# A graph layer and a small network on one core: a sort run earlier and in shorter pieces, weights on another queue, a finer last unit

## The chip, the core and the metric

The kernel runs on one core of a Trainium2 chip. The core has five engines with instruction streams of their own: TensorE (PE) multiplies matrices, VectorE (DVE) and ScalarE (ACT) work elementwise, GpSimd (POOL) prepares indirect memory accesses here, and SyncE (SP) only issues DMAs. An engine executes its instructions strictly in order, and waits at one whose inputs are not there. DMAs can be issued from SP's, ACT's and POOL's queues and are carried out by 16 DMA engines.

The metric is the time of one execution on the device in microseconds (us). For the kernel before, three runs gave 1962.46, 1963.09 and 1964.54: the median is 1963.09 us.

## What is computed

```python
def gnn(x, weight, row, col, vals):
    h = jnp.einsum('nf,ef->ne', x, weight)
    return jax.ops.segment_sum(vals[:, None] * h[col], row, num_segments=8192)

def ffn(x_bd, W, b):                      # W: 7 layers of 160 x 160
    mask = (x_bd[..., 0] >= 0.5) & (x_bd[..., 1] >= 0.5)
    ...                                   # two 4-bit numbers per row read from columns 64 to 111
    for i in range(7):
        h = jnp.einsum('bspd,ed->bspe', h, W[i]) + b[i]
        if i < 6: h = jax.nn.relu(h)
    ...                                   # one result per position, rounded, clipped to 0..15
    return x_bd with 2 * one_hot(result) added in columns 128 to 159 where mask

x = x + gnn(layernorm(x), L0_gnn_weight, src, dst, edge_weight)
x = x + ffn(layernorm(x)[None], L0_ffn_W, L0_ffn_b)[0]
```

x has 8192 rows of 512 floats; there are 131072 edges with a source row, a target row and a weight. For each edge one row of h, chosen by dst, is multiplied by the weight and summed into row src. The edges arrive sorted by dst, but the sum goes by src, so the kernel has to sort them by blocks of 128 rows of src itself.

## The kernel before

The 8192 rows are 64 blocks of 128. The work has three stages, and the order of PE, DVE and ACT is written out by hand with Python generators: each `yield` marks a place where another stream's instructions may be put in.

**Heads and first sort.** `project()` makes h block by block (a "head"). Two blocks of x come in by one DMA; `scale` takes mean and variance on DVE (L431, L432), the reciprocal deviation on ACT and DVE (L183, L184) and scales on ACT (L437); `turn` transposes on PE (L446) with a copy on ACT (L448); four matmuls (L464) and a copy (L466) give h, which SP stores to DRAM two blocks at a time (L468). `order(part)` sorts the edges of one part: for each chunk of edges, `chunk` works out a one-hot of the block (`hot`, L238), its running counts (L246, L248, L251, L252), the rank by PE (L257, L261), the slot (`at`, L265), and puts the edges into cells by matmuls (`blocks`, L274; `put`, L278; L289). After seven chunks for part 0 or nine for part 1, `squeeze` moves the filled cells together in ten rounds (L351 to L359, all on DVE but one copy), then PE transposes the result into the tables `at_dst`, `at_row` and `at_w` (L393, L395). A head is followed by 1.25 steps of the first sort, from head 5 on.

**Part 0 with the second sort.** Each block takes 6 tiles of 128 edges in part 0 and 11 in part 1: 384 and 704 tiles in all. For each tile POOL gathers 128 rows of h by an indirect DMA (L723) into `g`, DVE makes a weighted one-hot `hot` (L734, seven batches of four tiles ahead), and PE multiplies them into `p_g` (L750). A tiny matmul for each batch, the "join" into `p_j` (L748), reads one element of each of the four gathered tiles. `g` has six buffers of four tiles. A finished block is added to x on DVE (L768) and stored. After every fourth tile one step of the second sort follows.

**Part 1 with the network.** The blocks continue with 11 tiles each; the sum is added to the stored rows (L807) and the network `ffn` runs over units of eight blocks, one step after every fifth tile. It gathers the rows that need it into 128 columns and takes six layers (L523 to L534 on PE, L506 on DVE, L509 on ACT) and an output. Then eight instructions on ACT scale the unit's rows (L630), two on DVE add the result (L651), and SP stores 2 MB (L654).

At the start ACT issues the DMA for the graph weight (L153), then those of the network's weights (L165 to L173), and copies some of them to their places (L174 to L179) before its first instruction of a head.

Of the kernel before, what the change touches and what calls it, by code (L numbers as in the profile page):

```python
# [24 lines left out]
OPVAL = 2 + 27  # L25
# [8 lines left out]
def tile_gnn_ffn(  # L34
# [49 lines left out]
    GS = 4  # L84
    assert E % P == 0 and D == 512 and NB == 64 and N <= 1 << DSTS and LOW + BITS <= 31
# [79 lines left out]
    nc.scalar.dma_start(w_a, ffn_wT[:, :P, :].rearrange("l d e -> d l e"))  # L165
    for g in range(NG):
        gs = slice(GB * g, GB * (g + 1))
        nc.scalar.dma_start(w_b[gs], ffn_wT[:, P:, :].rearrange("l d e -> d l e"))
        for i, d in enumerate(GE_IN):
            nc.scalar.dma_start(w_in[GB * g + i : GB * g + i + 1, 0, :], ffn_wT[0, d : d + 1, :])  # L170
        nc.scalar.dma_start(b_b[gs], ffn_bT[P:, :])
    nc.scalar.dma_start(b_a, ffn_bT[:P, :])
    nc.scalar.dma_start(b_out, ffn_bT[RESULT : RESULT + 1, L - 1 : L].to_broadcast([P, 1]))  # L173
    nc.scalar.copy(wo_a[:, 0, 0:1], w_a[:, L - 1, RESULT : RESULT + 1])  # L174
    nc.scalar.copy(wo_b[:, 0, 0:1], w_b[:, L - 1, RESULT : RESULT + 1])
    for g in range(NG):
        gs = slice(GB * g, GB * (g + 1))
        nc.scalar.copy(w_z[gs, 1:, g, :], w_b[gs, 1 : L - 1, 0:P])
        nc.scalar.copy(w_z[GB * g : GB * g + 3, 0, g, :], w_in[GB * g : GB * g + 3, 0, 0:P])  # L179

    def rstd_of(pool, var_ap, n, name):
        r = pool.tile([P, n], F32, name=name)
        nc.scalar.activation(r, var_ap, AF.Sqrt, bias=eps)  # L183
        nc.vector.reciprocal(r, r)  # L184
        return r

# [25 lines left out]

    with tc.tile_pool(name="ld", bufs=1) as ld:
# [21 lines left out]
    def chunk(ck, ps_c, q, col):  # L235

        hot = ck.tile([P, GC, NB, GQ], BF16, name="hot")
        nc.vector.tensor_tensor(  # L238
            hot, each.rearrange("p (o b) g -> p o b g", o=1).to_broadcast([P, GC, NB, GQ]),
            blk[:, q].rearrange("p c (o g) -> p c o g", o=1).to_broadcast([P, GC, NB, GQ]),  # L240
            OP.is_equal)
        yield
# [6 lines left out]
        yield  # L249
        for c in range(1, GC):  # L250
            nc.vector.tensor_tensor(cum[:, c], cum[:, c - 1], hot[:, c - 1], OP.add)  # L251
        nc.vector.tensor_tensor(cum, cum, hot, OP.mult)  # L252
        yield
        p_rank = ps_c.tile([P, GC, NB // GC, GQ], F32, name="p_rank")
        nb = NB // GC
        for i in range(GC):
            nc.tensor.matmul(p_rank, eye, cum[:, :, i * nb : (i + 1) * nb, :], start=(i == 0),  # L257
                             stop=(i == GC - 1))
        yield
# [5 lines left out]
        nc.vector.tensor_tensor(  # L265
            at.rearrange("p n h s -> p n (h s)"),
            lots.rearrange("p (o h) s -> p o (h s)", o=1).to_broadcast([P, CG, CAP]),
            slot.to_broadcast([P, CG, CAP]), OP.is_equal)
        p_c = None
        for c0 in range(0, GC, SUB):  # L270
            cg = slice(c0 * GQ, (c0 + SUB) * GQ)
            n = SUB * GQ
            blocks = ck.tile([P, SUB, GQ, NB], F32, name="blocks", bufs=2)
            nc.scalar.copy(blocks, hot[:, c0 : c0 + SUB].rearrange("p c b g -> p c g b"))  # L274
            put = ck.tile([P, n, 2, 2, HALF], F32, name="put", bufs=2)
            for i, val in enumerate((val_a, val_w)):
                v = val[:, q, c0 : c0 + SUB, :].rearrange("p c (g a b) -> p (c g) a b", a=1, b=1)
                nc.vector.tensor_tensor(put[:, :, :, i, :], at[:, cg],  # L278
                                        v.to_broadcast([P, n, 2, HALF]), OP.mult)
            yield  # L280
# [4 lines left out]
            for k in range(n):  # L285
                c, g = divmod(k, GQ)
                last = c0 + SUB == GC and k == n - 1
# [7 lines left out]
    def squeeze(part, sq, ps_q):  # L295
# [7 lines left out]
        nc.vector.tensor_tensor_scan(dist, free, free, 0.0, op0=OP.add, op1=OP.max)  # L303
# [8 lines left out]
        yield  # L312
# [5 lines left out]
        nc.vector.tensor_tensor(dist, dist, free, OP.mult)  # L318
        nc.vector.tensor_copy(word, cells_a[:, :ROW])
        yield  # L320
        nc.vector.tensor_copy(far, dist)
        nc.vector.scalar_tensor_tensor(word, far, LOW, word, op0=OP.logical_shift_left,
# [158 lines left out]
    for _ in heads:  # L481
        pass
    for _ in first:
        pass
# [542 lines left out]
```

## Time and profile before

| what | us |
|---|---|
| median of three runs | 1963.09 |
| the profiled execution, its own time | 1969.51 |
| its span, first to last instruction | 1967.7 |
| PE busy | 1686.7 (86%) |
| DVE busy | 982.7 (50%) |
| ACT busy | 388.9 (20%) |
| POOL busy | 1143.2 (58%) |

Rows of the profile name an engine, a line, an operation and the tiles (out<-in). A group has its count, its busy time and mean duration in ns, then the engine's idle time before such instructions and what ended it. The page also cuts the span in 40 slices; a digit is the busy share in tenths:

```profile
PE   3999999667989899996687789898998989899994
DVE  2555655865556565659923333534434443434412
POOL 2000000007778787778877777777777777777750
```

The first nine slices, of 49 us each, are the heads with the first sort; then come some twelve of part 0, and the rest is part 1. POOL's work, apart from setting constants in the first slice, is the gathers alone. Issuing a DMA from SP or ACT is not counted as busy.

### The profile page before, as it was taken

How to read it: one execution, taken by the hardware profiler on the slowest of the kernel's cores; microseconds unless marked ns; L12 is line 12 of the kernel's file. 1: busy time of each engine (PE TensorE's matmuls, PEld its weight loads, DVE VectorE, ACT ScalarE, POOL GpSimd, SP SyncE). 2: the span in 40 equal slices, each digit the busy share in tenths (PEclk: the TensorE clock that was granted, in tenths of full speed). 3: DMA queues.
4: the chain of work that ended last, by engine and by line, in shares of the span. 5: the costliest groups of instructions: out<-in, count | busy, mean ns of one | idle time of the engine just before them, and what ended most of it. 6: DMA issues, size and time to landing. Idle time of an engine off the chain costs nothing. (4 is left out here: it accounts for less than half of the span.)

```text
span 1967.7 us, 24257 instructions
## 1 busy us (share of the span) xinstructions
PE 1686.7 (86%) x9389; PEld 806.8 (41%) x9389; DVE 982.7 (50%) x2318; ACT 388.9 (20%) x513; POOL 1143.2 (58%) x1115
## 2 busy tenths in 40 slices
PE   3999999667989899996687789898998989899994
PEld 1555555323445454442233334343433434343442
DVE  2555655865556565659923333534434443434412
ACT  3545555331112111111100001010010101001012
POOL 2000000007778787778877777777777777777750
PEclk9999999888999899998899999999999999999997
DMA  4322222126777777776689777878787787878761
GB/s 152 101 72 86 86 87 86 65 75 197 241 235 249 235 227 245 228 243 191 189 242 348 210 209 210 296 209 296 208 270 228 217 288 210 294 211 252 207 216 45
DMA packets 141826, 391.38 MB, mean 199 GB/s; under 512 B 20220, under 2 KB 22024, under 8 KB 141704
## 3 DMA queue, kind: packets, MB, share of 16 engines
q0 software_dynamic: 87040, 285.28, 48.1%
q1 hardware_dynamic: 51760, 102.25, 14.8%
q10 hardware_dynamic: 2904, 2.21, 0.4%
q8 instruction: 78, 1.28, 0.3%
q14 instruction: 44, 0.36, 0.1%
HBM read 339.33 MB, written 50.33 MB: 198 GB/s over the span
## 5 line engine op out<-in xcount | busy, mean ns | idle before, releaser
L723 POOL DMA_INDIRECT g<-h_rows,at_dst x1088 | 1133.3, 1042 | 763.5 <-issue 717.8
L750 PE MATMUL p_g<-g,hot 128*128 128x512 f32 x2176 | 1066.7, 631 | 0.0
L750 PEld LDWEIGHTS p_g<-g,hot 128*128 128x128 f32 x2176 | 404.4, 198 | 405.8 <-issue 394.2
L734 DVE TENSOR_SCALAR hot<-lanes,at_row,at_w 128x128 f32<-128x128 f32 x1088 | 301.9, 359 | 177.0 <-PE p_g L750 160.3
L464 PE MATMUL p_g<-xg,g 128*128 128x512 f32 x512 | 243.5, 620 | 3.6 <-ACT g L448 3.5
L748 PE MATMUL p_j<-g,hot 128*1 128x4 f32 x544 | 52.6, 168 | 178.4 <-DMA g<-h_rows,at_dst 176.7
L274 ACT CAST blocks<-hot 128x1024 f32<-128x1024 bf16 x64 | 131.5, 2077 | 210.4 <-PE p_c L289 210.4
L748 PEld LDWEIGHTS p_j<-g,hot 128*1 128x1 f32 x544 | 26.5, 80 | 344.4 <-issue 331.3
L289 PEld LDWEIGHTS p_c<-put,blocks 128*64 128x64 f32 x4096 | 125.9, 139 | 51.9 <-issue 36.7
L289 PE MATMUL p_c<-put,blocks 128*64 128x40 f32 x4096 | 133.4, 231 | 8.9 <-ACT blocks L274 7.4
L464 PEld LDWEIGHTS p_g<-xg,g 128*128 128x128 f32 x512 | 97.2, 200 | 105.8 <-issue 99.3
L506 DVE TENSOR_SCALAR hb<-p_b,b_b 128x128 f32<-128x128 f32 x48 | 16.8, 351 | 219.1 <-PE p_b L526 189.1
L768 DVE TENSOR_TENSOR xg<-xg,p_g 128x512 f32<-128x512 f32 x64 | 43.8, 684 | 97.3 <-PE p_g L750 97.2
L446 PE MATMUL p_g<-ident,g 128*128 128x128 f32 x256 | 43.3, 296 | 56.2 <-ACT g L437 56.2
L278 DVE TENSOR_TENSOR put<-at,val_a 128x640 f32<-128x640 bf16 x64 | 52.7, 824 | 67.2 <-PE p_c L289 66.6
L807 DVE TENSOR_TENSOR xu<-xu,p_g 128x512 f32<-128x512 f32 x64 | 43.7, 683 | 83.2 <-PE p_g L750 83.0
L509 ACT ACTIVATE ha<-p_a,b_a 128x512 f32<-128x512 f32 x48 | 33.0, 687 | 260.4 <-PE p_a L534 250.3
L251 DVE TENSOR_TENSOR cum<-cum,hot 128x512 bf16<-128x512 bf16 x112 | 47.7, 426 | 64.6 <-ACT cum L248 61.3
L183 ACT ACTIVATE rstd_f<-mv_f,eps 128x8 f32<-128x8 f32 x8 | 2.4, 302 | 374.5 <-DVE mv_f L702 374.5
L446 PEld LDWEIGHTS p_g<-ident,g 128*128 128x128 f32 x256 | 31.5, 149 | 75.4 <-issue 42.4
L466 ACT COPY g<-p_g 128x512 f32<-128x512 f32 x64 | 37.4, 585 | 114.8 <-PE p_g L464 114.8
L278 DVE TENSOR_TENSOR put<-at,val_w 128x640 f32<-128x640 bf16 x64 | 52.4, 818 | 0.0
(173 smaller groups left out, 1044.7 us busy)
## 6 DMA issues: line engine op xcount, KB each, us to landing
g<-h_rows,at_dst POOLq DMA_INDIRECT x1088, 3.9
g<-in_x_dram SPq DMA_DIRECT2D x32, 512.0 KB
xg<-in_x_dram SPq DMA_DIRECT2D x16, 1024.0 KB
h_rows<-g SPq DMA_DIRECT2D x32, 512.0 KB
x_rows<-xg SPq DMA_DIRECT2D x32, 512.0 KB
xu<-x_rows SPq DMA_DIRECT2D x16, 1024.0 KB
out_dram<-xu SPq DMA_DIRECT2D x8, 2048.0 KB
xg<-in_gnn_wT_dram ACTq DMA_DIRECT2D x1, 1024.0 KB
```

The costliest lines, as they stand in the source:

```text
L251: nc.vector.tensor_tensor(cum[:, c], cum[:, c - 1], hot[:, c - 1], OP.add)
L274: nc.scalar.copy(blocks, hot[:, c0 : c0 + SUB].rearrange("p c b g -> p c g b"))
L278: nc.vector.tensor_tensor(put[:, :, :, i, :], at[:, cg], v.to_broadcast([P, n, 2, HALF]), OP.mult)
L289: nc.tensor.matmul(p_c[h * NB : (h + 1) * NB, g], blocks[:, c, g, :], put[:, k, h], start=False, stop=last)
L446: nc.tensor.transpose(p_t[:, k * P : (k + 1) * P], t[:, 2 + b % 2, k * P : (k + 1) * P], ident)
L464: nc.tensor.matmul(p_h, t[:, b % 2, k * P : (k + 1) * P], gw[:, k, :], start=(k == 0), stop=(k == KD - 1))
L723: nc.gpsimd.indirect_dma_start(out=g[:, k, :], out_offset=None, in_=h_rows, in_offset=bass.IndirectOffsetOnAxis(ap=at_dst[part][:, i : i + ...
L734: nc.vector.tensor_scalar(hot[:, k, :], lanes, at_row[part][:, i : i + 1], at_w[part][:, i : i + 1], op0=OP.is_equal, op1=OP.mult)
L748: nc.tensor.matmul(p_j[:, part, :], hot[:, GS - 1, 0:1], g[:, :, 0], start=(m == 0), stop=(m == NBUF[part] - 1))
L750: nc.tensor.matmul(p_g, hot[:, i, :], g[:, i, :], start=(k == 0), stop=(k == TILES[part] - 1))
L768: nc.vector.tensor_add(xg[:, b % G, :], xg[:, b % G, :], p_g)
L807: nc.vector.tensor_add(xj, xj, p_g)
```

## The change

1. **Weights.** The 23 DMAs of the network's weights are issued from POOL's queue instead of ACT's, and ACT's copies of them move into a function that is called after the last head.
2. **First sort.** It begins at head 2 and takes two steps a head in the chunks and one a head in the squeeze, whose rounds now have two steps. When it is finished, the batches of `hot` for the first seven gathers are made beside the remaining heads.
3. **Second sort.** In part 1's chunks DVE's long instructions are cut in eight (`put` in two), in its squeeze in four. `due` counts tiles: a chunk's step every 3 tiles, a squeeze's every 4.
4. **Join.** The matmul reads its operands as bfloat16, upper halves of the same words, instead of float32.
5. **Network.** ACT's scaling of a unit's rows is spread over the layers' steps. The last unit of eight blocks becomes two of four, with half the columns and a step every 2 tiles; the very last stores columns 160 to 511 as soon as they are scaled, and the first 160 after the result.

```diff
-    nc.scalar.dma_start(w_a, ffn_wT[:, :P, :].rearrange("l d e -> d l e"))
+    nc.gpsimd.dma_start(w_a, ffn_wT[:, :P, :].rearrange("l d e -> d l e"))
     ...
+    def spread_weights():
+        nc.scalar.copy(wo_a[:, 0, 0:1], w_a[:, L - 1, RESULT : RESULT + 1])
     ...
+    def cut(n, parts):
+        return [slice(n * i // parts, n * (i + 1) // parts) for i in range(parts)]
     ...
-        nc.vector.tensor_tensor(cum, cum, hot, OP.mult)
-        yield
+        for cs in cut(GC, parts):
+            nc.vector.tensor_tensor(cum[:, cs], cum[:, cs], hot[:, cs], OP.mult)
+        yield STEP
     ...
-            nc.vector.scalar_tensor_tensor(stay[:, :n], go[:, :n], -1, word[:, :n],
-                                           op0=OP.bitwise_xor, op1=OP.bitwise_and)
-            nc.vector.copy_predicated(stay[:, :m], go[:, s : m + s], word[:, s : m + s])
             w2 = sq.tile([P, ROW], F32, name="w2", bufs=2)
             nc.scalar.copy(w2[:, :n], wt[:, :n])
-            nc.vector.copy_predicated(w2[:, :m], go[:, s : m + s], wt[:, s : m + s])
+            for cs in cut(n, parts):
+                nc.vector.scalar_tensor_tensor(stay[:, cs], go[:, cs], -1, word[:, cs],
+                                               op0=OP.bitwise_xor, op1=OP.bitwise_and)
+            yield SLOW
+            for to, of in ((stay, word), (w2, wt)):
+                for cs in cut(m, parts):
+                    ds = slice(cs.start + s, cs.stop + s)
+                    nc.vector.copy_predicated(to[:, cs], go[:, ds], of[:, ds])
     ...
-        qs, col = (range(QA), 0) if part == 0 else (range(QA, NQ), CARRY)
+        qs, col, fine = (range(QA), 0, 1) if part == 0 else (range(QA, NQ), CARRY, GC)
     ...
-                yield from chunk(ck, ps_c, q, col)
+                yield from chunk(ck, ps_c, q, col, fine)
     ...
-            yield from squeeze(part, sq, ps_q)
+            yield from squeeze(part, sq, ps_q, (fine + 1) // 2)
     ...
-    LEAD, MORE, LESS = 5, 5, 4
-    for b in range(NB):
-        next(heads)
-        if b >= LEAD:
-            for _ in range((b + 1) * MORE // LESS - b * MORE // LESS):
-                next(first, None)
     ...
+    LEAD, MORE = 2, 2 * STEP
+    credit, early = 0, 0
+    for b, _ in enumerate(heads):
+        credit += MORE if b >= LEAD else 0
+        while credit > 0 and first:
+            n = next(first, None)
+            if n is None:
+                first = None
+            else:
+                credit -= n if n == STEP else MORE
+        if first is None and early < AHEAD:
+            hots_for(early)
+            early += 1
     ...
+    spread_weights()
     ...
-            if t % STEP == STEP - 1:
-                next(second, None)
+            if t == due:
+                due += next(second, NB * FT)
     ...
-                    nc.tensor.matmul(p_j[:, part, :], hot[:, GS - 1, 0:1], g[:, :, 0],
+                    nc.tensor.matmul(p_j[:, part, :], hot[:, GS - 1, :].bitcast(BF16)[:, 1:2],
+                                     g.rearrange("p k d -> p (k d)").bitcast(BF16).rearrange(
+                                         "p (k d) -> p k d", k=GS)[:, :, 1],
     ...
+        units = [(b, U) for b in range(0, NB - U, U)] + [(NB - U, U // 2), (NB - U // 2, U // 2)]
     ...
+                    settle(n // 4)
+                    if early and not left:
+                        nc.sync.dma_start(rows_of(out, b0, n)[:, :, end:], xu[:, :, end:])
     ...
-        for j in range(U):
-            nc.scalar.activation(xu[:, j, :], xu[:, j, :], AF.Identity,
-                                 bias=nmr[:, j : j + 1], scale=up[:, j : j + 1])
     ...
+        if early:
+            nc.sync.dma_start(rows_of(out, b0, n)[:, :, :end], xu[:, :, :end])
+        else:
+            nc.sync.dma_start(rows_of(out, b0, n), xu)
     ...
-                if (b * TILES[1] + k) % EVERY == EVERY - 1:
+                every = 5 if units[u][1] == U else 2
+                if (j * TILES[1] + k) % every == every - 1:
                     step()
```

STEP is 3, SLOW is 4; GC is 8, so `fine` is 8 for the second sort and 1 for the first.

## The prediction

> **What bounds the kernel now.** I read the windows of 50 us first, because the page's busy shares (PE 86%, POOL 58%) average three different stages; then the listing of instructions in order of time at the borders of the stages. In the windows the columns are PE, PEld, DVE, ACT and POOL busy (with counts), the clock, the DMA share and GB/s.
>
> ```profile
> 300.00:350.00 50.00, 46.39 (x448) 27.23 (x445) 26.93 (x46) 25.49 (x37) 0.00 (x0) 0.97 0.26 86
> 350.00:400.00 50.00, 35.09 (x90) 15.68 (x89) 45.71 (x60) 19.39 (x29) 0.00 (x0) 0.86 0.21 70
> 400.00:450.00 50.00, 25.34 (x69) 11.43 (x67) 29.69 (x70) 13.48 (x24) 6.79 (x6) 0.80 0.28 86
> 600.00:650.00 50.00, 46.46 (x422) 24.86 (x422) 30.49 (x62) 9.65 (x9) 39.64 (x35) 0.97 0.78 243
> 900.00:950.00 50.00, 28.34 (x60) 11.30 (x60) 49.59 (x60) 8.99 (x6) 42.38 (x26) 0.86 0.58 176
> 1200.00:1250.00 50.00, 46.52 (x194) 20.70 (x193) 20.03 (x64) 7.69 (x11) 37.81 (x41) 0.97 0.78 248
> ```
>
> See POOL: no gather before 441.69, then 41 gathers in a quiet window, 35 beside the second sort, 26 at 900. The listing explains the numbers (start, duration, engine, line, what; in brackets the idle time before):
>
> ```profile
> 442.50 2.29 DVE L238 TENSOR_TENSOR hot<-each,blk 128x4096 bf16<-128x4096 bf16 x1
> 443.18 2.44 POOL L723 DMA_INDIRECT g<-h_rows,at_dst  x1 [0.30 <-issue]
> 445.92 0.95 POOL L723 DMA_INDIRECT g<-h_rows,at_dst  x1 [0.30 <-issue]
> 447.17 0.95 POOL L723 DMA_INDIRECT g<-h_rows,at_dst  x1 [0.30 <-issue]
> ```
>
> A gather undisturbed takes 0.95 and the next begins 0.30 later: 1.254 per gather, back to back, from 441.69 to 1907.43. The gather that met L238 (running to 444.79) stood still until then and needed 0.83 more: stretched by 1.49. The page has the mean of all 1088:
>
> ```profile
> L723 POOL DMA_INDIRECT g<-h_rows,at_dst x1088 | 1133.3, 1042 | 763.5 <-issue 717.8
> ```
>
> 1042 - 948 = 94 ns x 1088 = 102 us of such stretching. So the span is a sum of POOL's times: 441.7 (first gather) + 1087 x 1.254 + 0.95 = 1364 + 102 + 60.3 (1907.4 to 1967.7) = 1968. In part 1 the mean is 950 ns, so all 102 lie in the 384 gathers of part 0. PE is near, not over: it only waits for landings.
>
> **Start and first sort.**
>
> ```profile
> 14.35 0.18 DVE L432 BATCH_NORM_AGGREGATE mv_h<-st_h 128x2 f32<-128x6 f32 x1
> 25.04 1.28 ACT L174 ACT_TABLE_LOAD   x1 [25.04 <-DMA w_in<-in_ffn_wT_dram]
> 33.23 1.94 PE L446 MATMUL p_g<-ident,g 128*128 128x128 f32 x8 [33.23 <-ACT g L437]
> ```
>
> The statistics of x are ready at 14.5, but ACT issues 23 weight DMAs until 25.0, then spreads weights until 30.3. With both gone, rstd, scale and the first transpose follow as now (1.7 us after rstd): PE at 16.5, **-16.7**. On POOL's queue the 23 DMAs follow its last memset (10.3) and stand before the first gather, with 400 us of cover; even at 3 us each they would hide. They still share DMA engines (45% busy in the first 50 us) with x, whose third load SP issued at 23.63: should it come late, heads 3 and 4 lose a few us. The ten copies (4 x (0.72 + 0.29) + 0.4 = 4.4 us) move behind the last head, beside the 7.8 us from the last h store (433.91) to the first gather. They become free only if the weights land in 400 us.
>
> A head (four transposes, four matmuls) costs PE 3.87 (39.63 to 43.50); a chunk 12.3 (L246 1.9, L257 1.9, L283 0.3, L289 8.3). Before: five heads, 1.25 steps a head, chunks 41.6 us apart; then the squeeze from 347.89, where 14 heads carry 75 us of DVE and PE falls to 35 and 25 per 50. After: three heads, two steps a head, so a chunk has four: 4 x 3.87 + 12.3 = 27.8, over the clock 0.96 = 29. Only one head now stands between L246 and L257 and between L257 and L289; the trace has both cases, where PE idled 2.4 us each. With them 34 a chunk, 7 x 34 = 238. Then 27 pieces of the squeeze, one a head: DVE at most 2.1 + 2.8 + 1.6 of statistics per two heads, below PE's 8, so 27 x 4.0 = 108. Then seven batches of hots (8.3 us at 434.30 now) beside the last six heads, 24. Sum: 16.5 + 6.4 (first head) + 7.7 + 238 + 108 + 2 + 24 = 402.5, + 8 (store) = **410.5** for the first gather, -31. Ends: 395 (chunks without stalls) and 425 (only the start is won).
>
> **Part 0 with the second sort.** Cut pieces give POOL openings. Seven adds of 0.43 (L251, back to back) already show what a piece costs: the 1.05 and 1.07 gathers under them; over the stage 12 gathers lost 1.5 us. The stretch is the rest of the running instruction less 0.13.
> [...]
> [...] The trace gives 2.29 for 4096 and 0.43 for 512, thus 0.16 fixed; but four independent hots take 1.11, not 4 x 0.36, so 0.10 of it overlaps. 29 more pieces a chunk are [...]1.7 by the row; I take 1.7. Of DVE's time 20 + 9.5 (hots, adds) per 36 that is no bound; it lengthens the chains by 0.5.
>
> What becomes late next is **PE**. Steps come every 3 tiles instead of 4, 24 a chunk. Four tiles with their join take 3.75 (1911.72 to 1915.47), of which matmuls are 3.42; the one-pass join drops one of two passes, 0.15. So 6 x 3.6 = 21.6, + 12.3, + stalls: L246's end to L252's end is 6.2 in the trace, 6.7 cut, against 5.4 of tiles; rank to put is 5.9 against 5.4: 1.7 together. 35.6 / 0.97 = 36.6 a chunk, nine = 329. POOL alone would need 24 x 1.254 = 30, so it now waits for buffers: six of four tiles, so when PE has done 216 tiles (9.5 + 329 = 339 after the first gather) POOL has issued about 236, worth 296. **Lost 43**; stretches inside are hidden in it. Ends: 24 (no stalls) to 84 (40 a chunk).
> Squeeze: a bit is 0.97 + 1.79 + 1.90 + 1.88 = 6.5 of DVE, cut 7.1, with hots 2.1 and adds 0.9 10.1 in 8 tiles = 10.0 (before, 4 tiles: the 49.59). Balanced, and the seven batches of hots ahead cover some 35 us. [...] Residual stretch: 0.11 for a cut piece, 0.36 under the uncut L351, over 80 gathers 8; the start of the squeeze 2. **10**. Together 53 for the 102.
>
> **Part 1** (704 x 1.254 = 883) stays POOL's: PE 176 x 3.6 + 163 (all FFN rows) = 797. The join and ACT's spread of the L630 instructions win nothing there.
>
> **Tail.**
>
> ```profile
> 1906.49 0.94 POOL L723 DMA_INDIRECT g<-h_rows,at_dst  x1 [0.30 <-issue]
> 1919.34 0.69 DVE L807 TENSOR_TENSOR xu<-xu,p_g 128x512 f32<-128x512 f32 x1 [10.50 <-PE p_g L750]
> 1956.02 0.29 DVE L651 SCALAR_TENSOR_TENSOR xu<-p_v,xu 128x128 f32<-128x128 f32 x1 [2.35 <-ACT xu L630]
> 1957.04 0.38 SPq L654 DMA_DIRECT2D out_dram<-xu  x1
> ```
>
> Last gather to last add 11.9, then FFN 37.7, then store 10.7. With four blocks: ln -1.1, small DVE and p_v -1.3, layers 3.2 to about 2.3 each (512 columns become 256), -5.5; the wait for L630 -2.3: 28 if half rate (5.2 for the first layers, as now) lasts no longer. The store is 328 KB instead of 2 MB, the other 352 columns going some 10 us earlier: 5.3. Before it the denser last two units (20 + 12 of FFN in 88 tiles) keep PE about level with POOL; 11 stays. **44** for 60.3; ends 40 and 51.
>
> **Sum** against the profiled span 1967.7: 410.5 + 1364 + 53 + 44 = 1871.5, -96. The median shown is 1963.09, 4.6 below that span (the profiled execution itself 1969.51): forecast **1867**.
>
> **Rivals.**
> A, *the lock goes from piece to piece*: POOL finds no opening. 102 x 1.1 stays: 1867 + 59 = 1926. Against it the 0.1 under L251. 7%.
> B, *stage one no denser*: two steps a head only trade stalls, as the in-order queues do when DVE is late (L257, 2.4); first gather at 425: 1882. 18%.
> C, *PE keeps up*: no stalls, join nearly free, lost 15: 1829 to 1840. 12%.
> D, slower: *the sort's steps turn serial*. Each step waits for the last on DVE or ACT while PE, in order, stands with the tiles behind it. Then a chunk is 21.6 + its whole chain (2.7 + 1.9 + 0.6 + 6.2 + 1.9 + 6.3 + 8.5, with puts 5) = 55; lost 9 x 55 + 9.5 - 296 = 208: about 2022. It decides against the change from 47.5 us a chunk. For it: more instructions and fewer tiles between them. Against: in part 0 PE idled before no L257 or L289. 5%.
> Forecast case 58%: 1845 to 1892. Range to 1914, down to 1833, leaving most of A and D out. Within 0.2% (4 us, what a measurement can tell) needs two rivals at once: 1%; slower 6%; faster 93%.
>
> **Signs.** Right: first transpose near 16, first gather near 410; POOL rows of 0.95 to 1.2 beside cut pieces, but gaps over 0.30 "<-PE p_g" in the second sort, which before had none; PE over 46 per 50 there; the tail 44. Wrong: first gather past 425; 2 us gathers remaining; gathers that stop at number 384 because the sort is unfinished; chunks over 40 us apart.

## The result, and the profile after

The changed kernel takes **1926.7 us** (median of four runs, 1925.37 to 1930.34) against 1962.78 for the kernel before: a ratio of 0.9819, with a 95% interval of 0.9802 to 0.9836. The sign of the forecast was right. Its size was not: 36 us were won where 96 were forecast, and the time lies outside the range. The profiled execution took 1927.51 us, its span is 1925.7 us. In four of the six sets of experiments below the kernel before itself took 2225 to 2249 us instead of 1963, on one chip 2225.37 in one set and 1964.41 in a later one, so times are compared within a set alone, and each set is named by its time of the kernel before.

The page's slices and its group of the gathers, after (an engine's busy share in tenths of 48 us slices; then count, busy time, mean ns, idle time):

```profile
PE   5888889969999999878878789898988989899996
POOL 4000000017777777887777777777777777777760
L519 POOL DMA_INDIRECT g<-h_rows,at_dst x1088 | 1101.9, 1013 | 743.4 <-issue 691.6
```

The first slice of PE is 5 instead of 3: the late start is gone. POOL still begins in the ninth slice. The gathers' mean is 1013 ns instead of 1042; the forecast had nearly all of the excess over 948 going.

The windows of 50 us, in the columns of the prediction's table:

```profile
300.00:350.00 50.00, 49.97 (x150) 24.02 (x149) 41.37 (x63) 28.61 (x48) 0.00 (x0) 1.00 0.38 127
600.00:650.00 50.00, 47.58 (x478) 25.48 (x476) 41.22 (x115) 13.32 (x9) 38.43 (x36) 1.00 0.79 242
800.00:850.00 50.00, 33.14 (x56) 12.73 (x55) 44.77 (x105) 7.50 (x5) 42.08 (x27) 0.76 0.67 208
```

At 300 to 350 PE is full, as planned. At 600 it has 47.6 of 50, so the second sort is bound by PE. At 800, in the second squeeze, POOL is busy 42 us and makes only 27 gathers in 50 us: they are still long, 1.56 us on the mean, although VectorE's instructions are short now.

The forecast's sum, term by term, against the span:

| term | forecast | measured | difference |
|---|---|---|---|
| first gather starts | 410.5 | 427.1 | +16.6 |
| second sort's chunks: time over 1.254 us a gather | 43 | 40.7 | -2.3 |
| second squeeze: the same | 10 | 37.6 | +27.6 |
| part 1 | 883 | 885.6 | +2.6 |
| from the last gather's end to the span's end | 44 | 53.1 | +9.1 |

(1088 gathers at 1.254 us are in both columns. The chunks are gathers 0 to 235, from 427.1 to 763.8; the squeeze is gathers 236 to 383, from there to 987.0.) The differences add up to 54 us, the gap between 1871.5 and 1925.7. So three terms were to be explained.

**The first stage.** What PE waited for between 20 and 420 us (total us, times, longest):

```profile
PE p_c L308 <- ACT blocks L288: 21.8, 14, 2.5
PE p_rank L271 <- DVE cum L266: 16.4, 7, 2.4
```

In each of seven chunks PE stops twice at L308, 1.6 us on the mean, and once at L271 for 2.3. The chunks come 35.3 us apart on the mean. From the first transpose to the last store of h this order takes 401.5 us (17.9 to 419.4), the order before 400.7 (33.2 to 433.9). The denser order won nothing; the start's 15.3 us are all that was won.

**The squeeze.** Instructions in order of time (start, duration, then what it is):

```profile
798.87 2.03 DVE L387 COPY_PREDICATED word<-go,word 128x391 int32<-128x391 int32 x4
799.05 4.55 POOL L519 DMA_INDIRECT g<-h_rows,at_dst  x1 [0.31 <-issue]
800.79 2.02 DVE L387 COPY_PREDICATED w<-go,w 128x391 f32<-128x391 int32 x4
```

Eight pieces follow one another from 798.87 to 802.81, each a little before its predecessor's end (four take 2.03 us, though each by itself takes 0.59). The gather that met the first piece ends at 803.60, 0.79 after the *last* of the eight. But the series of seven dependent adds at L264 lets gathers through. Of the gathers that began with over 0.5 us of a series left, the 19 under L264 were stretched by 0.15 us on average, with 2.26 us of the series left; the 11 under L387 by 1.93, with 2.82 left. Seven of these 11 were held to the end of the eighth piece. The other four, in two of the nine rounds that gathers met, went at the end of the piece that they had met; VectorE had stood idle right before these rounds, waiting for TensorE:

```profile
842.16 0.69 DVE L819 TENSOR_TENSOR xg<-xg,p_g 128x512 f32<-128x512 f32 x1 [5.06 <-PE p_g L804]
842.76 1.99 DVE L387 COPY_PREDICATED word<-go,word 128x384 int32<-128x384 int32 x4
843.45 1.15 POOL L519 DMA_INDIRECT g<-h_rows,at_dst  x1 [0.30 <-issue]
```

So the form, the dependence or what stands ahead of the series decides.

**The tail.** Windows of 8 us around the last layers:

```profile
1886.00:1894.00 8.00, 1.89 (x23) 1.20 (x22) 5.91 (x26) 0.32 (x2) 0.00 (x0) 0.84 0.01 2
1894.00:1902.00 8.00, 7.49 (x60) 5.94 (x59) 0.85 (x3) 2.69 (x5) 0.00 (x0) 0.50 0.01 3
```

PE idles ahead of the layers, its granted clock falls to 0.50, and it stays there through all of them: 3.82 us a layer.

### The profile page after: what moved, and what is told of

Read it like the earlier page. It is cut to its first block, busy times and chain, and to the rows that moved or that the text cites. A ratio compares the mean times of both kernels' runs of the same rounds, so it can differ in the third digit from the quotient of the medians.

```text
span 1925.7 us, 24263 instructions
## 1 busy us (share of the span) xinstructions
PE 1695.5 (88%) x9288; PEld 819.9 (43%) x9288; DVE 1008.2 (52%) x2710; ACT 389.3 (20%) x520; POOL 1124.8 (58%) x1138
## 4 chain that ended last, share of the span: by engine, by line
PE 40%; POOL 19%; DMA 17%; issue 12%; DVE 9%; ACT 3%; POOLq 0%; DVEq 0%; ACTq 0%; SPq 0%
POOL g L519 19%; DMA g<-h_rows,at_dst 16%; PE p_g L804 16%; PE p_g L492 10%; PE p_c L308 6%; DVE cum L264 2%; DVE cum L266 2%; PE p_g L474 2%; ACT blocks L288 1%; DVE at L281 1%; PE p_base L259 1%; PE p_a L603 1%; PE p_a L601 1%; DVE hot L530 1%; PE p_rank L271 1%
## 5 line engine op out<-in xcount | busy, mean ns | idle before, releaser
L519 POOL DMA_INDIRECT g<-h_rows,at_dst x1088 | 1101.9, 1013 | 743.4 <-issue 691.6
L804 PE MATMUL p_g<-g,hot 128*128 128x512 f32 x2176 | 1071.9, 630 | 1.3 <-DVE xg L819 1.3
L804 PEld LDWEIGHTS p_g<-g,hot 128*128 128x128 f32 x2176 | 400.5, 197 | 385.1 <-issue 371.7
L308 PE MATMUL p_c<-put,blocks 128*64 128x40 f32 x4096 | 140.4, 236 | 28.9 <-ACT blocks L288 21.8
L800 PE MATMUL p_j<-g,hot 128*1 128x4 bf16 x272 | 45.7, 168 | 135.9 <-DMA g<-h_rows,at_dst 95.6
L308 PEld LDWEIGHTS p_c<-put,blocks 128*64 128x64 f32 x4096 | 132.9, 145 | 70.6 <-ACT blocks L288 33.8
L800 PEld LDWEIGHTS <-hot 128*1 128x1 bf16 x272 | 21.6, 79 | 317.2 <-issue 284.6
L575 DVE TENSOR_SCALAR hb<-p_b,b_b 128x128 f32<-128x128 f32 (+1 forms) x54 | 18.2, 336 | 218.5 <-PE p_b L595 195.9
L264 DVE TENSOR_TENSOR cum<-cum,hot 128x512 bf16<-128x512 bf16 x112 | 47.7, 426 | 118.5 <-ACT cum L261 115.2
L295 DVE TENSOR_TENSOR put<-at,val_a 128x320 f32<-128x320 bf16 (+1 forms) x100 | 54.9, 578 | 59.1 <-PE p_c L308 58.9
L578 ACT ACTIVATE ha<-p_a,b_a 128x512 f32<-128x512 f32 (+1 forms) x54 | 34.5, 640 | 217.0 <-PE p_a L603 206.3
L603 PEld LDWEIGHTS p_a<-hb,w_z 128*128 128x128 f32 x360 | 51.8, 207 | 17.9 <-issue 16.7
L295 DVE TENSOR_TENSOR put<-at,val_w 128x320 f32<-128x320 bf16 (+1 forms) x100 | 55.2, 580 | 0.0
```

Of the source, the lines that this page charges most:

```text
L295: nc.vector.tensor_tensor(put[:, cs.start * GQ : cs.stop * GQ, :, i, :], at[:, (c0 + cs.start) * GQ : (c0 + cs.stop) * GQ], v.to_broadcast ...
L308: nc.tensor.matmul(p_c[h * NB : (h + 1) * NB, g], blocks[:, c, g, :], put[:, k, h], start=False, stop=last)
L519: nc.gpsimd.indirect_dma_start(out=g[:, k, :], out_offset=None, in_=h_rows, in_offset=bass.IndirectOffsetOnAxis(ap=at_dst[part][:, i : i + ...
L603: nc.tensor.matmul(p_a[:, g, :], w_z[:, i, g, :], last_hb, start=False, stop=((g + 1) * T % 512 == 0 or g == NG - 1))
L800: nc.tensor.matmul(p_j[:, part, :], hot[:, GS - 1, :].bitcast(BF16)[:, 1:2], g.rearrange("p k d -> p (k d)").bitcast(BF16).rearrange("p (k ...
L804: nc.tensor.matmul(p_g, hot[:, i, :], g[:, i, :], start=(k == 0), stop=(k == TILES[part] - 1))
```

## The experiments

The sets, by the time of the kernel before in them: 2228.67 (e1 to e4), 2248.66 (r_after, e5 to e7), 2225.37 (e8, e9), 2248.38 (e10, e11), 1965.28 (e12, e13) and 1964.41 (e14 to e17). e1 to e4, e12 and e13 were executed once each. The first stage, which ends before any gather, is as long in all of them (one and the same order had its first gather between 425.4 and 430.0, the other order below between 396.7 and 402.8); its times may be set side by side, to within some 6 us. e14_after, the changed kernel once more, took 1927.62 (0.9818 of its kernel before [0.979, 0.9845]); it is the measure of the last set.

### The start alone: e1_weights

The kernel before, with the weights' loads moved from ScalarE's queue to GpSimd's and the ten copies behind the heads; nothing else:

```diff
-    nc.scalar.dma_start(w_a, ffn_wT[:, :P, :].rearrange("l d e -> d l e"))
+    nc.gpsimd.dma_start(w_a, ffn_wT[:, :P, :].rearrange("l d e -> d l e"))
...
+    spread_weights()
```

> The kernel before with one part of the change alone: the weights on GpSimd's queue and ACT's copies of them behind the last head; the sort's order is the old one. Theory (the first sort's new order wins nothing, its added stalls of 2.4 us at L271 and L308 pay for the shorter squeeze): first transpose near 17.9, first gather at 426 to 428, as in the changed kernel (427.1), total about 1948. Rival (the new order is worth some 10 us, and the start is worth less than its 15): first gather at 433 or later, total 1955.

Measured: first matmul at 17.9, first gather at 425.4; the changed kernel has 17.9 and 427.1. The old order of heads and steps, started early, is as good as the new one. All that the first stage won is the start. The whole took 2194.93 us where the kernel before took 2228.67, and in this set that is less than e2, e3 and e4 took (2212.27, 2232.55 and 2215.68), which have the denser second sort besides: its chunks took 414.5 us here and 471 to 473 there. In this set the rest of the change cost time; more of that with r_after.

### Other steps between the heads: e5_heads, e15_heads

The changed kernel, with the order of chunk steps written out over four heads:

```diff
-    LEAD, MORE = 2, 2 * STEP
-    credit, early = 0, 0
+    early = 0
+    CHUNKS_END = 2 + 4 * QA
     for b, _ in enumerate(heads):
-        credit += MORE if b >= LEAD else 0
...
+        if b < 2 or first is None:
+            n = 0
+        elif b == 2:
+            n = 3
+        elif b < CHUNKS_END:
+            n = (4, 1, 1, 2)[(b - 2) % 4]
+        else:
+            n = 1
```

> The changed kernel, with the steps of a sort chunk of the first part spread otherwise over its four heads of h (3+1, 1, 1, 2 instead of 2, 2, 2, 2), so that one head stands between the last product of cum and the rank matmuls, and one between the first blocks and the p_c matmuls. Theory (the denser order won nothing because two adjacent steps make TensorE wait 2.3 us for cum at L271 and 2.5 us for the blocks at L308 in each of 7 chunks of 34.9 us, so that the period is that of the old order): the two waits go, the period falls to about 30.5, the first gather comes 30 us earlier (at about 397), and the whole is 25 to 30 us faster than the changed kernel. Rival (the waits stand in a stage whose length is set by something else, such as the heads' own chain through ScalarE and the clock): other waits take their place, the period stays at 34 to 35 and the first gather at 424 to 428.

> The kernel of e5_heads (steps of a chunk of the first part spread 3+1, 1, 1, 2 over its four heads). If the kernel before is near 1963: theory (the 28 us won before the first gather in e5_heads pass through to the end, since the gathers follow one another from there) first gather at 397 to 401, total 26 to 30 us below the changed kernel, so about 1898; rival (given back later) less than half of it.

Measured: e5_heads had its first gather at 399.0 and took 2224.28, 29.6 us less than the changed kernel in its set. e15_heads, in the set in which the kernel before took 1964.41 and the changed one 1927.62, had it at 402.7 and took **1899.16 us** (1895.43 to 1904.43), 0.9658 of the kernel before [0.9636, 0.968]. Its waits before the first gather, to be read beside those above:

```profile
PE p_rank L271 <- DVE cum L266: 16.5, 7, 2.4
PE p_c L308 <- ACT blocks L288: 7.4, 13, 0.6
```

One of the two waits went, from 21.8 to 7.4, and the chunks come 32.3 us apart instead of 35.3. The other stayed, as one chunk of e15_heads shows:

```profile
71.83 2.29 DVE L266 TENSOR_TENSOR cum<-cum,hot 128x4096 bf16<-128x4096 bf16 x1
74.18 1.04 PE L271 MATMUL p_rank<-cum,eye 128*128 128x512 bf16 x4 [2.35 <-DVE cum L266]
```

Between the matmuls of p_base, which end at 67.96, and those of p_rank stands one head, in both orders, and it keeps TensorE busy for 3.87 us. The chain of ScalarE's copy, VectorE's seven adds and its product takes 6.2, without a pause. The rest, 2.35 us, is the wait in each of the seven chunks, in the changed kernel and here alike. The first gather comes 24.0 us earlier than in e14_after: until then TensorE is idle for 14.6 us less and busy for 9.5 less, with the clock at half for 24 us instead of 38. The theory held for one wait out of two, and the gain passed through to the end: 28.5 us of medians.

### The squeeze's pieces: e3_uncut, e2_overlap

e3_uncut leaves the second squeeze whole (`squeeze(part, sq, ps_q, 1)`). e2_overlap keeps the pieces of the predicated copies but begins each one column early, so that it writes one column again that its predecessor wrote, and has to wait for it, which the rows below show:

```diff
                 for cs in cut(m, parts):
+                    cs = slice(max(cs.start - 1, 0), cs.stop)
                     ds = slice(cs.start + s, cs.stop + s)
                     nc.vector.copy_predicated(to[:, cs], go[:, ds], of[:, ds])
```

> The changed kernel with the squeeze's instructions whole again in the second sort (the chunks stay cut). Theory (the cut pieces of the predicated copies act as one long instruction): the loss between gather 236 and 384 stays at 35-45 us, total 1923-1936. Rival (the cut brings what the prediction gave it, some 24 us): 1950.

> The changed kernel; in the second sort's squeeze each piece of a predicated copy begins one column early, so it writes one element that the piece before has written (the same value) and has to wait for it. Theory (independent pieces run into one another on DVE by 0.1 us, and the gather then stays locked out until the last): gathers of 3 to 4.6 us disappear, the loss between gather 236 and gather 384 falls from 38 to 12-16 us, total 1902-1906. Rival (the squeeze is late because DVE is full, 45 of 50 us busy): about 1 us more DVE work a round makes it later, 1928-1940.

Stretch of gathers 236 to 383 in one set: 38.6 us whole (e3_uncut), 34.9 cut (in e4_warm, whose squeeze is that of the changed kernel), **11.1** with overlapping pieces. These gathers took 235.1, 236.3 and 222.0 us. Cutting the squeeze's instructions won 3.7 us of stretch; making each piece of the predicated copies wait took 24 away, of which 14 passed through in this set, where the gathers wait for TensorE besides. The rival, a squeeze late because VectorE is full, is out: the pieces take longer with the overlap, and the squeeze came sooner. The pieces look like this in e17_all below, which has the same edit (line numbers are one higher):

```profile
764.77 2.50 DVE L388 COPY_PREDICATED word<-go,word 128x391 int32<-128x391 int32 x4
765.72 1.06 POOL L520 DMA_INDIRECT g<-h_rows,at_dst  x1 [0.30 <-issue]
767.09 0.97 POOL L520 DMA_INDIRECT g<-h_rows,at_dst  x1 [0.30 <-issue]
767.17 2.50 DVE L388 COPY_PREDICATED w<-go,cells_w 128x391 f32<-128x391 int32 x4
```

The four pieces take 2.50 instead of 2.03, and gathers go through under them: 33 began under such a series in that kernel, stretched by 0.05 on average.

That the overlap frees the gathers is shown; that independence is what holds them is not. The pieces at L266, L281 and L381 need nothing of one another either and also begin some 0.08 us before their predecessor's end, yet let gathers through (stretched by 0.09, 0.06 and 0.13 on average in the first profile). And eleven profiles have the cut squeeze without the overlap: of the gathers that met one of the first seven pieces of a series, 77 of 82 were held to its end where VectorE had come to it without a pause, and none of 46 where it had just stood idle for 1.6 to 7.1 us. No run changed this alone, so why the overlap lets go stays open.

### The chunks' pieces: e6_chunk_whole, e9_whole_again, e16_whole

The changed kernel, with the second part's chunks whole on VectorE and the squeeze cut (`chunk(ck, ps_c, q, col, 1)`).

> The changed kernel, with the second part's chunks on VectorE in whole instructions again, as in the kernel before; the squeeze stays cut. Theory (in the chunk phase TensorE is the bound in the changed kernel, with 47.5 to 48.4 us busy of 50, and the cut freed the gathers from the chunk's long instructions): uncut, gathers are stretched again by some 30 to 40 us over gathers 0 to 236, but part of it lies in the time that they wait for TensorE anyway; the total is 5 to 20 us longer than the changed kernel. Rival (TensorE is the bound, cut or not): no difference above 3 us, so that the cut of the chunks was worth nothing either.

> The kernel of e6_chunk_whole once more (the second part's chunks whole on VectorE, the squeeze cut). If the kernel before is near 1963 here: theory (the cut chunks made TensorE the bound and freed the gathers) the stretch of gathers 0 to 236 comes back and the total is 5 to 20 us above 1926.7; rival (TensorE bounds the chunk phase either way) within 3 us of it. If the kernel before is near 2240: some 25 us below it, as in e6_chunk_whole.

> The kernel of e6_chunk_whole (the second part's chunks whole on VectorE, the squeeze cut). If the kernel before is near 1963: theory (the cut chunks made TensorE the bound and freed the gathers) 5 to 20 us above the changed kernel; rival (TensorE bounds the chunk phase either way) within 3 us of it. If near 2240: some 15 to 30 us below it.

Where the kernel before took 1964.41, e16_whole took **1954.81** (1952.94 to 1956.96; 0.995 [0.9934, 0.9965]), 27 us more than the changed kernel, above the 5 to 20 expected. A gather that met the whole L266:

```profile
448.22 2.29 DVE L266 TENSOR_TENSOR cum<-cum,hot 128x4096 bf16<-128x4096 bf16 x1
448.85 2.48 POOL L519 DMA_INDIRECT g<-h_rows,at_dst  x1 [0.30 <-issue]
```

Gathers 0 to 235 are stretched by 71.4 us in all instead of 33.5, and the stage takes 367.1 us instead of 336.2; the squeeze gives 6.9 back. These 27 us are more than the 21 that the change wins beyond its start: with the denser steps and without the cut, the second sort's chunks take 18 us longer than in the kernel before (367.1 and 348.6). In the set of 2248.66 the same edit made the kernel faster by 30 us (e6_chunk_whole 2223.75, changed kernel 2253.89), against the expectation; e9_whole_again took 2210.93, 0.9942 of its kernel before [0.9923, 0.996]. What TensorE does there comes with r_after.

### A warm TensorE: e4_warm, e7_all, e10_warmer

e4_warm puts 7 and then 4 small matmuls, of no use to the result, ahead of the last layers:

```diff
+            def warm(n):
+                p_w = ps_g.tile([P, D], F32, name="p_g")
+                for _ in range(n):
+                    nc.tensor.matmul(p_w[:, :256], ident, steps.rearrange("p a b -> p (a b)"),
+                                     start=True, stop=True)
...
             block(*last)
+            warm(7)
+            for _ in range(3):
+                step()
+            warm(4)
```

> The changed kernel with eleven matmuls more behind the last block whose output nobody reads: seven behind the last gathered tile, four while DVE prepares the last unit. Theory (the tail is long because TensorE's clock is at half for all of the last unit's layers): clock 1.0 in the tail, a layer 2.5 us instead of 3.82, last gather to end 45-47 us instead of 53, total 1919-1921. Rival (narrow matmuls cost this much at any clock, or the clock falls back in the layers however they begin): a layer stays at 3.8, total 1927.

Measured: the clock stays at 1.00, a layer takes 2.41 us instead of 3.82, and from the last add to the last computation it is 24.9 us instead of 33.5. e10_warmer has e7_all's edits with 10 and 5 such matmuls:

> The kernel of e7_all with 10 and 5 small matmuls ahead of the last layers instead of 7 and 4 (in e7_all and e8_all_again the clock fell to 0.50 in the layers in spite of them, with TensorE busy for 2.95 us of the 4 us before). Theory (the layers' period follows the clock, and the clock falls when TensorE idles ahead of them): clock 1.0 in the layers, period 2.4 instead of 3.82, the FFN part of the tail 25 instead of 32 to 33 us, total 8 us below what e7_all would take. Rival (the clock falls there by its own timing, as it also granted 0.8 and 0.9 in places with TensorE fully busy): period 3.8, no gain. If the kernel before is near 1963: about 1860.

There the clock fell all the same. Its windows of 4 us:

```profile
2156.50:2160.50 4.00, 4.00 (x26) 3.22 (x25) 3.28 (x17) 0.00 (x0) 0.00 (x0) 1.00 0.02 4
2160.50:2164.50 4.00, 3.41 (x46) 2.49 (x45) 0.91 (x4) 1.54 (x3) 0.00 (x0) 0.87 0.01 2
2164.50:2168.50 4.00, 3.74 (x28) 3.04 (x27) 0.28 (x1) 1.17 (x2) 0.00 (x0) 0.50 0.01 2
```

PE was busy for the whole of the 4 us before and 3.41 of the next 4, and fell. In e17_all it held with 6.97 of 8. Of the six kernels with such matmuls three kept the clock (e4_warm, e11_whole, e17_all) and three lost it (e7_all, e8_all_again, e10_warmer); all variants of the changed kernel without them lost it. That the period follows the clock is shown; that idling before the layers is what drops it isn't.

### All three, and the whole chunks: e7_all, e8_all_again, e17_all, e11_whole

One kernel with the heads' order of e5_heads, the pieces of e2_overlap and the matmuls of e4_warm.

> The changed kernel with three edits: the heads' steps as in e5_heads, the predicated pieces begun one column early as in e2_overlap, and the idle TensorE kept busy with 11 small matmuls ahead of the last layers as in e4_warm. Theory: the gains add up (28 of the first stage, 24 of the squeeze, 9 to 12 of the tail): 1926 - 62 = about 1864. Rival (each is given back at the next bound): less than half of that, 1895 or more.

> The kernel of e7_all once more, because the chips of the first two sets made the kernel before take 2229 and 2249 us (TensorE waits there within runs of short matmuls, with no engine to wait for, as soon as the gathers run), so that their totals can't be set against 1926.7. If the kernel before is near 1963 here: theory (the three gains stand at places that do not touch one another) 1926.7 - 28 - 24 - 10 = 1865, with the first gather at 399 to 403, 24 us less stretch over gathers 192 to 384, and a tail of 44 or less; rival (given back at the next bound) 1895 or more. If the kernel before is near 2240: again some 45 to 55 us below it.

> The kernel of e7_all (heads spread, predicated pieces begun one column early, 7 and 4 small matmuls ahead of the last layers). If the kernel before is near 1963: theory (the gains stand at places that do not touch one another) 28 of the first stage and 24 of the squeeze, so about 1875, and 8 less, 1867, where the clock holds in the last layers; rival (given back at the next bound) 1895 or more.

e17_all, beside 1964.41 and 1927.62: **1870.44 us** (1865.46 to 1874.27), 0.951 [0.9486, 0.9533] of the kernel before. It beats both kernels (e15_heads, with the heads' order alone, has 221.7 for the squeeze), and the profiles say where, against the changed kernel of the same set (1925.0 and 1872.4): first gather -24.2, squeeze 222.9 to 199.2, so -23.7, tail 52.6 to 46.6, so -6.0; the rest +1.3. Its tail:

```profile
1838.00:1846.00 8.00, 6.97 (x27) 4.56 (x26) 4.20 (x16) 0.30 (x1) 0.00 (x0) 1.00 0.00 0
1846.00:1854.00 8.00, 7.09 (x83) 5.37 (x81) 2.65 (x14) 2.71 (x5) 0.00 (x0) 1.00 0.02 4
```

PE is kept going, and the clock beside it is 1.00. The matmuls themselves delay the last add by some 2 us. e7_all and e8_all_again took 2199.88 and 2171.64, 0.977 [0.9729, 0.9811] and 0.9803 [0.9739, 0.9866] of their kernels before. That is 54 us below the changed kernel of the set for e7_all, which had been expected 62 below it, and 54 below the kernel before for e8_all_again, as expected.

e11_whole is e10_warmer with whole chunks:

> The kernel of e10_warmer with the second part's chunks whole on VectorE. If the kernel before is near 2240 [...]: 15 to 30 us below e10_warmer, as e6_chunk_whole and e9_whole_again were 15 to 30 us below the changed kernel, so some 80 us below the kernel before. If it is near 1963: 5 to 20 us above e10_warmer, because the gathers are the bound there and the whole instructions hold them.

Where the kernel before took 2248.38, e10_warmer took 2191.19 and e11_whole 2172.28 (0.9655 [0.9625, 0.9684]). By the profiled executions, 21.4 us apart, the tail is 5.8 us shorter in e11_whole, where the clock held, and the second sort 28.6 (gathers 0 to 235 took 454.1 us instead of 477.3, the squeeze 213.4 instead of 218.8); the first gather came 6.1 later, and part 1 took 7.0 longer.

### TensorE's stops: r_after, e12_half_bytes, e13_half_rows

> The changed kernel itself, as the common measure of this set: if the chip is as the one of the first comparison, 1926 us, first gather at 427, gathers 236 to 384 in 223 us, tail from the last gather's end to the span's end 53 us.

Measured: 2253.89 against 2248.66, a ratio of 1.002 [1.0007, 1.0034]: in this set the change wins nothing. The first stage is as long as ever (first gather at 427.4). The listing of TensorE in the second sort of r_after shows what is new:

```profile
578.63 1.45 PE L308 MATMUL p_c<-put,blocks 128*64 128x40 f32 x42 [0.85 <-DVE put L295]
580.50 0.20 PE L308 MATMUL p_c<-put,blocks 128*64 128x40 f32 x1 [0.42 <-issue]
581.23 0.32 PE L308 MATMUL p_c<-put,blocks 128*64 128x40 f32 x2 [0.53 <-issue]
```

A run of 64 matmuls, 2.07 us long elsewhere, breaks off again and again with nothing to wait for. Such stops within the runs of L308 add up to 62 us in r_after; the changed kernel's first profile has none. They are the smaller part of the difference. The span is 326.7 us longer than in that profile (2252.4 and 1925.7): TensorE is busy for 105.3 us more (1800.8 and 1695.5), with a mean granted clock of 0.890 instead of 0.952, and idle for 221.4 more. 158 of the 327 us lie in part 1, which has no such runs. There are longer stops too:

```profile
L308 PE MATMUL p_c<-put,blocks 128*64 128x40 f32 x4096 | 166.7, 239 | 110.1 <-issue 61.8
477.69 2.58 PE L308 MATMUL p_c<-put,blocks 128*64 128x40 f32 x44 [19.86 <-DVE put L295]
```

In the second of these lines put is late because VectorE stood until 471.95, waiting for ranks; the record of their last matmul ends at 452.24. What held the result in between the profile does not tell. (The first line is of the page.)

TensorE is then the bound, the gathers wait for its buffers (91 us at L804 between 430 and 800, where the changed kernel's first profile has 10), and to free the gathers from VectorE's long instructions was worth nothing. After the first, the second sort's chunks come 51.1 us apart in r_after, with whole ones in e6_chunk_whole 47.8; why the cut makes them longer there was not settled.

Two kernels were to tell whether the gathers' traffic is behind the stops, by its bytes or by its rows:

> The changed kernel, but each gather brings rows of 256 values instead of 512 (128 rows as before, half the bytes), and the aggregation's matmuls read these 256 columns twice, so that TensorE's work keeps its size. It leaves out half of h. On the chips of the study the kernel before takes 2225 to 2249 us instead of 1963, since TensorE stops for 0.6 us at a time within runs of short matmuls that wait for no engine: 66 us in all at the cells' matmuls, none before the first gather beyond 4.5. Theory [...]: with half the bytes the stops fall to half or less (below 35 us at the cells' matmuls) and the time to 2100 or less. Rival (it is the number of rows, [...]or the chip): the stops stay at 60 to 70 us and the time above 2200.

> The changed kernel, but each gather brings 64 rows of 512 values instead of 128 (half the bytes and half the rows), and the aggregation's matmuls contract over these 64 partitions. It leaves out half of the edges. Theory of traffic: the stops fall as in e12_half_bytes, by the bytes. Theory of rows [...]: they stay in e12_half_bytes and fall here. If neither falls, the stops come from something that the gathers do not set.

In their set the kernel before took 1965.28, so there were no stops to reduce, and the question is open. e12_half_bytes took 1921.23: with half the bytes the gathers of part 1 took 883.8 us instead of 885.6, so their bytes are no bound. e13_half_rows took 2099.47, longer with less to move: its clock stands at 0.5 for ten slices of the page in which TensorE is busy 90% or more. What in it lowered the clock was not tried.

## Why the prediction was wrong

**The start: right.** "PE at 16.5" came at 17.9; the activation table (1.28 us, from 14.96) is still loaded only when the first statistics are there, at 14.87. The weights on GpSimd's queue cost nothing that shows: the last of them is issued by 27.3, and the first gather starts at 427.1.

**Step "7 x 34 = 238 ... 27 x 4.0 = 108 ... 24": the stage's term, 16.6 us too small.** Of these, 1.4 are the start, 8 the chunks (246 us in all) and 7 the last 33 heads (140.9 instead of 134). The mechanism was seen: both waits of 2.4 us were in the forecast. What was missed is that with them the new order is no denser than the old one. Rival B named this with its number, "first gather at 425"; it had 18%. e1_weights shows it, and e15_heads what another order brings: 24 us at the first gather.

**Step "43": right, 40.7, with two errors that cancel.** The chunk came at 36.4 instead of 36.6. The one-pass join (272 records of 0.168 us, before 544) won nothing (four tiles with a join take 3.73, before 3.75; 0.15 was booked six times a chunk), and the clock was 1.00 instead of 0.97. That PE becomes the bound here, with waits of 1.8 us a chunk at L271 and L308, was forecast and came: 33 of the 40.7 us are stretched gathers, and TensorE waited for none of them between 450 and 750. e16_whole shows what the cut is worth, 27 us. Whole L251, L266 and L281 each held gathers by some 2 us there: in two rows by 1.53 (2.48 instead of 0.95, at 448.85 under L266) and 2.60 (3.55, at 454.14 under L281). What in these instructions holds a gather was not shown.

**Step "Residual stretch: 0.11 for a cut piece": wrong, 27.6 us.** This is the step that failed. It was taken from L251 of the kernel before (L264 now), seven adds of which each needs the result of the last. The pieces of the predicated copies need nothing of one another, and in seven of the nine rounds that gathers met, one that meets a piece is held to the end of the last. The trace of before had that form in it, in two whole copies:

```profile
911.65 1.96 DVE L356 COPY_PREDICATED word<-go,word 128x1566 int32<-128x1566 int32 x1
912.74 3.43 POOL L723 DMA_INDIRECT g<-h_rows,at_dst  x1 [0.30 <-issue]
913.51 1.87 DVE L359 COPY_PREDICATED w<-go,w 128x1566 f32<-128x1566 int32 x1
```

This gather ended 0.79 us after the second copy, which needs nothing of the first; one more was held so, and seven others went at the end of the first copy. Rival A, "the lock goes from piece to piece", was true for two forms, the predicated copies at L387 and the hot pieces at L251 (8 of 8 gathers stretched, by 2.07 us on average, hidden there because PE was the bound); it was false for L264, L266, L281 and L381. That its sum, 1926, is the measured time is luck: it put 59 us more into the second sort, where 25 came; the rest are the first stage and the tail. The nearest row had been chosen by its kind of cost and not by what ties one piece to the next. e2_overlap added that tie and nothing else, and the stretch went from 34.9 to 11.1.

**Step "28 if half rate lasts no longer": 6 us too small, and 2.5 for the last add.** The half rate lasted through all layers, at 3.82 us instead of the 2.3 taken. The forecast held on to the trace of before, where only the first layers were slow: the half rate began at 1921.4 there and was over at 1938.5. Here it began at 1891.4 and lasted to the end, with TensorE busy for 3.74 of every 4 us in the layers in both. Why the clock did not rise again stays open. e4_warm gives 24.9 us at the full clock. The early store was right (5.6 for 5.3).

**Part 1: right.** 885.6 for 883; the gathers remain the bound.

With the three terms mended, e17_all stands at 1870.44, beside the forecast of 1867. Its terms are not all those of the forecast: the first gather at 402.5 instead of 410.5 makes up for the squeeze (13.6 instead of 10) and the tail (46.6 instead of 44). The sum was right in its structure; what it took for granted in three places had to be built first.

## What to carry to other kernels

Before an instruction is cut so that others can get in between, look whether its pieces depend on one another; where they don't, they may act as one, as the predicated copies did (4.55 us for a gather of 0.95), and here an overlap of one column made them let go (34.9 us of stretch became 11.1). Two steps that depend on each other across engines belong on either side of other work, and that work has to be as long as the chain between them: one head of 3.9 us against a chain of 6.2 left a stall of 2.35 in every chunk. And what a cut is worth depends on which engine is the bound: leaving the same chunks whole cost 27 us where the gathers then set the pace, and saved 30 in the set in which TensorE was it.

## What was not expected of the hardware

- A series of independent predicated copies (4 of 391 columns, 2.03 us) held a gather until all eight pieces had run in seven of nine rounds, and not in the two before which VectorE had stood idle; the same pieces, each waiting for the last, held none (0.05 us).
- In some sets TensorE stops for about 0.6 us at a time within runs of matmuls of 40 columns while gathers run, 62 us in all in r_after, and now and then for much longer (19.86 us at 457.8); r_after takes 2254 us instead of 1927.
- The granted clock fell to 0.50 in e10_warmer within 8 us in which TensorE was busy for 7.41, stayed there for 20 us at 3.74 busy of 4 (the changed kernel), and was 0.5 for long in e13_half_rows with TensorE busy 90% or more.
